# Selective scan: both channel halves in one two-bank PSUM tile, with softplus, delta times u and the turned copies as single operations

## The chip, the cores and the metric

The kernel runs on one core of a Trainium2 chip. The metric is device time in microseconds of one execution; three executions of the kernel before gave a median of 18506.04 us (18495.7 to 18506.94). The kernel has four layers in a row; the change lies in the scan of the last one.

## What is computed

The input is an image batch of 2 x 128 x 128 pixels with 128 channels. Layers 0 to 2 (window attention, a Fourier layer, a gated iteration) are not touched. Layer 3 is a selective scan in four directions over 256 channels. Cut to the part in question:

```
x_dbl = einsum('bkdl,kcd->bkcl', xs, x_proj_w)         # 4 directions k
dts, Bs, Cs = split(x_dbl, [8, 24], axis=2)
delta = softplus(einsum('bkrl,kdr->bkdl', dts, dt_proj_w) + dt_bias)
step:   h = exp(delta * A) * h + (delta * u) * B        # 16 states per channel
        y = sum over states of h * C
y = y + u * D;  the four directions are turned back and added
```

L is 16384 pixels, and each direction runs through them in its own order, two of them (k = 0, 1) forth and two (k = 2, 3) back.

## The kernel before, in words

`layer3_scan` (L1219) cuts each direction of each image into 32 parts of 512 pixels: 256 parts in all, in 8 blocks of 32, a block of "forth" parts (k below 2) and a block of "back" parts (k of 2 or 3) by turns. 256 channels times 16 states are 32 groups of 128 rows, so each part has 32 scans of 128 x 512. They are made in 8 slots of 4 (`tiles`, L1578): for each scan PE turns four 128 x 128 blocks of products `but` into a PSUM tile `ups` (L1591), and DVE scans it with the decay factors `da` into `hs` (L1599). `ups` has three buffers.

Around a scan slot g stands the rest of the recurrence, written out in the loop at L1623:

```
at(g, "head"); exponentials(g+1); kept(g-1); at(g, "mid")
products(g+2); weighted(g-1); tiles(g); sums(g-2); at(g, "end")
```

- `exponentials` (L1528): ACT makes `da`, four operations of 128 x 512.
- `kept` (L1605): ACT copies the last column of the four scans into `states`. It waits for the scans of slot g-1.
- `products` (L1540): `but` = delta times u, times B, 8 operations of 128 x 256, of which ACT does six or seven and POOL one or two.
- `weighted` (L1613): POOL multiplies `hs` by C in place, one operation of 128 x 2048.
- `sums` (L1563): PE sums over the states into two PSUM banks `yps`.

`in_order` (L114) ties every engine to the order in which this code issues, so nothing overtakes anything on its engine. Each part also has steps that run at fixed slots beside the scans of an earlier or later part. The list at L1508 gives (slot relative to the part's first, place in the slot, step); a place 0 to 3 is after that scan of the slot. By the slot of the eight in which they fall, with the engine that does the work:

| slot | steps |
|---|---|
| 6 | `project` (PE, `xdps`, places 1 and 2); `store` of a back part (ACT, head: two copies `yt<-ytps`, L1501) |
| 7 | `projected` (ACT, head: `xd`) |
| 0 | `turn_b` (PE, `btps`, 0), `ranks` 0 and 1 (PE, `dtps`, places 1 and 2) |
| 1 | `softplus_a` (ACT, head: two Abs out of `dtps`, L1366, and an Exp), `turned_b` (DVE, 0), `softplus_b` (DVE, 2), `skip` 0 (DVE, 3) |
| 2 | `softplus_c` (ACT, mid: Ln), `softplus_d` 0 and 1 (DVE, L1387, 0 and 1), `softplus_e` 0 and 1 (DVE, L1394, 2 and 3), `skip` 1 (DVE, 3) |
| 3 | `softplus_f` 0 and 1 (DVE, L1403, 0 and 1), `spread` (DMAs by SP, 2) |
| 4 | `turn` 0 and 1 (PE, `dltps`, L1430, 0 and 1) |
| 5 | `turned` 0 and 1 (DVE, `du` = `ut` times `dltps`, L1440, 0 and 1); `unturn` 0 and 1 of a back part (PE, `ytps`, L1491, places 2 and 3) |

PSUM has eight banks here: three `ups`, two `yps`, and three in `ps_m` (L1243). All small results (`xdps`, `btps`, the two `dtps`, the two `dltps`, the two `ytps`) are one-bank tiles of one tag in that pool, and take its three buffers by turns: a new tile waits until the last reader of the tile that had its buffer is done.

## Time and profile before

| | us |
|---|---|
| median of three executions | 18506.04 |
| the profiled execution | 18497.56 |
| its span, first to last instruction | 18495.8 |
| scan stage: first scan starts, last scan starts | 6302.4, 17972.4 |
| DVE, ACT, POOL busy between 8000 and 10000 (2000 us) | 1957.68, 1953.05, 1947.89 |
| PE busy in the same stretch | 1552.42 |

The profile page gives busy time by engine, by slices of the span and by group of instructions. The timeline lists instructions in order with their start, their length and, in brackets, the idle time of the engine before them and what ended it; a run of like instructions is one line. Lengths overlap: an instruction's tail lies under the next one's start, so what an instruction takes of its engine is the distance from its start to the next start, where the engine doesn't wait. In what follows that distance is called its step. The list of waits sums who waited for whom in a stretch.

### The profile page before, as it was taken

How to read it: one execution, taken by the hardware profiler on the slowest of the kernel's cores; microseconds unless marked ns; L12 is line 12 of the kernel's file. 1: busy time of each engine (PE TensorE's matmuls, PEld its weight loads, DVE VectorE, ACT ScalarE, POOL GpSimd, SP SyncE). 2: the span in 40 equal slices, each digit the busy share in tenths (PEclk: the TensorE clock that was granted, in tenths of full speed). 3: DMA queues.
4: the chain of work that ended last, by engine and by line, in shares of the span. 5: the costliest groups of instructions: out<-in, count | busy, mean ns of one | idle time of the engine just before them, and what ended most of it. 6: DMA issues, size and time to landing. Idle time of an engine off the chain costs nothing. (4 is left out here: it accounts for less than half of the span.)

```text
span 18495.8 us, 280256 instructions
## 1 busy us (share of the span) xinstructions
PE 14497.6 (78%) x98938; PEld 8455.1 (46%) x98938; DVE 15999.1 (87%) x20731; ACT 14932.9 (81%) x30141; POOL 11956.1 (65%) x6710
## 2 busy tenths in 40 slices
PE   7888888887567777777777777777777777777778
PEld 5665666674223344444444444444444444444445
DVE  6666666335888899999999999999999999999996
ACT  4665666333445799999999999999999999999984
POOL 0000000011000399999999999999999999999981
PEclk9999999889779899999999998999999989999999
DMA  2000000121114544444444454544444444455546
GB/s 49 23 23 22 16 16 16 55 72 55 49 48 147 174 119 119 118 126 126 127 114 119 120 128 126 126 118 116 120 126 127 126 122 115 116 122 128 132 129 191
DMA packets 1228553, 1861.32 MB, mean 101 GB/s; under 512 B 120781, under 2 KB 587469, under 8 KB 1224846
## 3 DMA queue, kind: packets, MB, share of 16 engines
q1 hardware_dynamic: 1157374, 1817.40, 37.2%
q10 hardware_dynamic: 69776, 26.00, 0.6%
q8 instruction: 785, 12.86, 0.3%
q14 instruction: 618, 5.06, 0.1%
HBM read 1398.48 MB, written 444.60 MB: 100 GB/s over the span
## 5 line engine op out<-in xcount | busy, mean ns | idle before, releaser
L1599 DVE TENSOR_TENSOR_SCAN hs<-da,states,ups 128x512 f32<-128x512 f32 x8192 | 9920.7, 1262 | 248.9 <-PE ups L1591 235.9
L1617 POOL TENSOR_TENSOR hs<-hs,cb 128x2048 f32<-128x2048 f32 x2048 | 9406.4, 4593 | 310.1 <-POOL but L1554 185.2
L1591 PE MATMUL ups<-ident,but 128*128 128x128 f32 x32768 | 5576.7, 301 | 2578.9 <-DVE hs L1599 1718.8
L1591 PEld LDWEIGHTS ups<-ident,but 128*128 128x128 f32 x32768 | 3873.7, 151 | 6179.9 <-DVE hs L1599 3526.1
L1559 ACT ACTIVATE but<-du,bt 128x256 f32<-128x256 f32 x12800 | 5328.7, 497 | 4.7 <-DVE du L1440 4.2
L1535 ACT ACTIVATE da<-db,na 128x512 f32<-128x512 f32 x8192 | 5224.1, 710 | 19.1 <-DMA db<-dd 17.8
L1573 PE MATMUL yps<-hs,sel 128*32 128x512 f32 x16384 | 2495.2, 685 | 60.7 <-POOL hs L1617 48.2
L1554 POOL TENSOR_TENSOR but<-du,bt 128x256 f32<-128x256 f32 x3584 | 2148.8, 620 | 15.2 <-DVE du L1440 15.2
L282 POOL TENSOR_TENSOR xres<-xres,rowb 128x256 f32<-128x256 f32 x128 | 93.2, 728 | 2641.3 <-DMA xres<-in_x 2512.5
L390 ACT COPY pT<-tps 128x512 f32<-128x512 f32 x1280 | 723.8, 586 | 1123.3 <-PE tps L385 1123.3
L385 PE MATMUL tps<-ident,s 128*128 128x128 f32 x8192 | 1180.8, 283 | 367.5 <-DVE pT L388 273.2
L358 DVE CUSTOM_DVE_ANT_0 s<-sps,relbias 128x512 f32<-128x512 f32 x2048 | 1321.6, 683 | 114.6 <-PE sps L342 109.2
L385 PEld LDWEIGHTS tps<-ident,s 128*128 128x128 f32 x8192 | 889.0, 142 | 898.8 <-issue 486.0
L370 ACT ACTIVATE s<-s,nm 128x1024 f32<-128x1024 f32 x1024 | 1163.5, 1137 | 85.3 <-DVE nm L368 82.1
L1130 POOL MEMSET xpad<- 128x34 f32 x8 | 1.3, 162 | 1242.5 <-PE xs L1021 1178.1
L1611 ACT COPY states<-hs 128x4 f32<-128x4 f32 x2048 | 380.9, 186 | 274.9 <-DVE hs L1599 274.7
L342 PE MATMUL sps<-kc,qT 32*128 32x512 f32 x4096 | 596.7, 650 | 0.8 <-DVE nm L358 0.8
L388 DVE COPY pT<-tps 128x512 f32<-128x512 f32 x768 | 526.6, 686 | 55.0 <-PE tps L385 54.5
L1573 PEld LDWEIGHTS yps<-hs,sel 128*32 128x32 f32 x16384 | 340.7, 114 | 486.0 <-issue 309.6
L1323 PE MATMUL xdps<-xc,xpw 128*40 128x512 f32 x1024 | 541.4, 611 | 12.3 <-POOL xd L1260 12.3
L1355 PE MATMUL dtps<-xd,dtw 65*128 65x512 f32 x1024 | 535.6, 605 | 0.0
L725 POOL TENSOR_TENSOR xr<-xr,row_ln_b 128x512 f32<-128x512 f32 x64 | 81.2, 1270 | 701.5 <-ACT acc L687 353.5
(286 smaller groups left out, 16784.7 us busy)
## 6 DMA issues: line engine op xcount, KB each, us to landing
db<-dd SPq DMA_DIRECT2D x1024, 512.0 KB
cb<-cd SPq DMA_DIRECT2D x1024, 256.0 KB
xc<-xs SPq DMA_DIRECT2D x256, 512.0 KB
dd<-dl SPq DMA_DIRECT2D x256, 512.0 KB
ut<-xst SPq DMA_DIRECT2D x128, 512.0 KB
yc<-ysb SPq DMA_DIRECT2D x128, 512.0 KB
yf<-yc SPq DMA_DIRECT2D x128, 512.0 KB
ys<-yt SPq DMA_DIRECT2D x128, 512.0 KB
```

The source lines that it names most:

```text
L342: nc.tensor.matmul(sps, v["qT"][hp, qt * P : (qt + 1) * P], kc[b, wh + g][hp, :, c0 : c0 + 32], start=True, stop=True,)
L358: nc.vector.tensor_tensor_reduce(v["s", qt][:, h, cols], v["sps", qt, g][h], bias[:, qt, h, cols], op0=ALU.add, op1=ALU.min, scale=-1.0, s ...
L370: nc.scalar.activation(s[:, h, :], s[:, h, :], AF.Exp, bias=nm[:, 2, h : h + 1], scale=-1.0, accum_out=v["sums"][:, qt, h : h + 1],)
L385: nc.tensor.transpose(tps[:, j, :], v["s", qt][:, h, k0 : k0 + P], cs.ident)
L390: nc.scalar.copy(dst, tps)
L1535: nc.scalar.activation(da[:, j, :], held[i]["db"][:, 4 * e + j, :], AF.Exp, scale=na[:, k, c : c + 1])
L1554: nc.gpsimd.tensor_tensor(but[:, j, :, n, :], du[:, tb], bt[:, tb, c : c + 1].unsqueeze(2).to_broadcast([P, 8, 32]), ALU.mult,)
L1559: nc.scalar.activation(but[:, j, :, n, :], du[:, tb], AF.Copy, scale=bt[:, tb, c : c + 1])
L1573: nc.tensor.matmul(v["yps"][e][32 * j : 32 * j + 32, :], sel, hs[:, j, :], start=(q == 0), stop=(q == 3),)
L1591: nc.tensor.transpose(ups[:, tb * P : (tb + 1) * P], v[("but", q, tb // 2)][:, tb % 2, 4 * e + j].rearrange("p n c -> p (n c)"), cs.ident,)
L1599: nc.vector.tensor_tensor_scan(o, a, u, state[:, c0 + j : c0 + j + 1], ALU.mult, ALU.add)
L1617: nc.gpsimd.tensor_tensor(hs, hs, v["cb"][:, s // 2, :].unsqueeze(1).to_broadcast([P, 4, T]), ALU.mult)
```

## The change

The pool `ps_m` gets one buffer for each tag instead of three. The tag "misc" keeps `xdps` and `btps`; a new tag "pair" holds one tile of two banks, shared by turns by `dtps`, `dltps` and `ytps`. The operations that ran once for each bank run once for both: `softplus_a`'s Abs, `softplus_d`, `_e`, `_f`, `turned` and `store`'s copy. Matmuls and transposes stay as they are, and write halves of the tile. Operations that came at places 0 and 1 (or 2 and 3) come at the first of them.

```diff
-        ps_m = pool("l3b_ps_m", 3, space=PSUM)
+        ps_m = pool("l3b_ps_m", 1, space=PSUM)
...
+        def two_banks(i, name):
+            return ps_m.tile([P, 2, T], F32, name=f"{name}_{tag_of(i)}", tag="pair")
...
         def ranks(e):
-                ps = ps_m.tile([P, T], F32, name=f"dtps_{tag_of(i)}_{e}", tag="misc")
+                if e == 0:
+                    v["dps"] = two_banks(i, "dtps")
                 nc.tensor.matmul(
-                    ps, dtw[:, k, e * P : (e + 1) * P], v["xd"], start=True, stop=True
-                )
-                v.setdefault("dps", []).append(ps)
+                    v["dps"][:, e], dtw[:, k, e * P : (e + 1) * P], v["xd"], start=True, stop=True
+                )
...
         def softplus_a(i):
-            for e in range(2):
-                nc.scalar.activation(ae[:, e, :], v["dps"][e], AF.Abs)
+            nc.scalar.activation(ae, v["dps"], AF.Abs)
             nc.scalar.activation(ae, ae, AF.Exp, scale=-1.0)
...
-                nc.vector.scalar_tensor_tensor(ps, ps, 0.0, v["ae"][:, e, :], ALU.max, ALU.add)
+            nc.vector.scalar_tensor_tensor(ps, ps, 0.0, v["ae"], ALU.max, ALU.add)
...
-                nc.vector.scalar_tensor_tensor(
-                    ps, v["up"][:, e, :], -1.0, ps, ALU.add, ALU.subtract
-                )
+            nc.vector.scalar_tensor_tensor(ps, v["up"], -1.0, ps, ALU.add, ALU.subtract)
...
-                nc.vector.tensor_tensor(dl, dl, v["dps"][e], ALU.subtract)
+            nc.vector.tensor_tensor(v["dl"], v["dl"], v["dps"], ALU.subtract)
...
         def turn(g):
-                tps = ps_m.tile([P, 2, 2, P], F32, name=f"dltps_{tag_of(i)}_{g}", tag="misc")
+                if g == 0:
+                    v["tps"] = two_banks(i, "dltps")
...
-        def turned(g):
-                nc.vector.tensor_tensor(
-                    v["du"][:, 2 * g : 2 * g + 2, :], v["ut"][:, 2 * g : 2 * g + 2, :],
-                    v["tps"][g].rearrange("p j e d -> p j (e d)"), ALU.mult,
-                )
+        def turned(i):
+            nc.vector.tensor_tensor(flat(v["du"]), flat(v["ut"]), flat(v["tps"]), ALU.mult)
...
         def unturn(g):
-                tps = ps_m.tile([P, 2, 2, P], F32, name=f"ytps_{tag_of(i)}_{g}", tag="misc")
+                if g == 0:
+                    v["ytps"] = two_banks(i, "ytps")
...
         def store(i):
-            for g in range(2):
-                nc.scalar.copy(
-                    yt[:, 2 * g : 2 * g + 2, :], v["ytps"][g].rearrange("p j e d -> p j (e d)")
-                )
+            nc.scalar.copy(flat(yt), flat(v["ytps"]))
             nc.sync.dma_start(pixels_of(i), yt)
...
-            (-6, "mid", softplus_c), (-6, 0, softplus_d(0)), (-6, 1, softplus_d(1)),
-            (-6, 2, softplus_e(0)), (-6, 3, softplus_e(1)),
-            (-5, 0, softplus_f(0)), (-5, 1, softplus_f(1)), (-5, 2, spread),
-            (-4, 0, turn(0)), (-4, 1, turn(1)), (-3, 0, turned(0)), (-3, 1, turned(1)),
+            (-6, "mid", softplus_c), (-6, 0, softplus_d), (-6, 2, softplus_e),
+            (-5, 0, softplus_f), (-5, 2, spread),
+            (-4, 0, turn(0)), (-4, 1, turn(1)), (-3, 0, turned),
```

In the order of issue this takes four DVE instructions out of every part (1024 in all) and 384 ACT instructions out of the scan (one Abs in each of 256 parts, one copy in each of 128 back parts). PE, POOL and SP keep their instructions and their order. Among the semaphore waits, the first transpose of `unturn(0)` gets a wait on DVE that it didn't have; before, `unturn(1)` had one.

More of the change, by code (lines that the diff above doesn't have):

```diff
@@ L1380, in softplus_c, with softplus_d, softplus_e, softplus_f @@
             v["dl"] = dl
-        def softplus_d(e):
-            def f(i):
-                v = held[i]
-                ps = v["dps"][e]
-                nc.vector.scalar_tensor_tensor(ps, ps, 0.0, v["ae"][:, e, :], ALU.max, ALU.add)
-            return f
-        def softplus_e(e):
-            def f(i):
-                v = held[i]
-                ps = v["dps"][e]
-                nc.vector.scalar_tensor_tensor(
-                    ps, v["up"][:, e, :], -1.0, ps, ALU.add, ALU.subtract
-                )
-            return f
-        def softplus_f(e):
-            def f(i):
-                v = held[i]
-                dl = v["dl"][:, e, :]
-                nc.vector.tensor_tensor(dl, dl, v["dps"][e], ALU.subtract)
-            return f
+        def softplus_d(i):
+            v = held[i]
+            ps = v["dps"]
+            nc.vector.scalar_tensor_tensor(ps, ps, 0.0, v["ae"], ALU.max, ALU.add)
+        def softplus_e(i):
+            v = held[i]
+            ps = v["dps"]
+            nc.vector.scalar_tensor_tensor(ps, v["up"], -1.0, ps, ALU.add, ALU.subtract)
+        def softplus_f(i):
+            v = held[i]
+            nc.vector.tensor_tensor(v["dl"], v["dl"], v["dps"], ALU.subtract)
         def spread(i):
@@ L1429, in f @@
                         p0 = (2 * g + j) * P
-                        nc.tensor.transpose(tps[:, j, e, :], v["dl"][:, e, p0 : p0 + P], cs.ident)
-                v.setdefault("tps", []).append(tps)
-            return f
-        def turned(g):
-            def f(i):
-                v = held[i]
-                if g == 0:
-                    v["du"] = two.tile([P, 4, 256], F32, name=f"du_{tag_of(i)}", tag="du")
-                nc.vector.tensor_tensor(
-                    v["du"][:, 2 * g : 2 * g + 2, :], v["ut"][:, 2 * g : 2 * g + 2, :],
-                    v["tps"][g].rearrange("p j e d -> p j (e d)"), ALU.mult,
-                )
-            return f
+                        nc.tensor.transpose(
+                            v["tps"][:, g, 256 * j + P * e : 256 * j + P * e + P],
+                            v["dl"][:, e, p0 : p0 + P], cs.ident,
+                        )
+            return f
+        def turned(i):
+            v = held[i]
+            v["du"] = two.tile([P, 4, 256], F32, name=f"du_{tag_of(i)}", tag="du")
+            flat = lambda a: a.rearrange("p t d -> p (t d)")
+            nc.vector.tensor_tensor(flat(v["du"]), flat(v["ut"]), flat(v["tps"]), ALU.mult)
         def load_forth(i):
@@ L1490, in f @@
                         p0 = (2 * g + j) * P
-                        nc.tensor.transpose(tps[:, j, e, :], v["ysb"][:, e, p0 : p0 + P], cs.ident)
-                v.setdefault("ytps", []).append(tps)
+                        nc.tensor.transpose(
+                            v["ytps"][:, g, 256 * j + P * e : 256 * j + P * e + P],
+                            v["ysb"][:, e, p0 : p0 + P], cs.ident,
+                        )
             return f
@@ L1499, in store @@
             yt = one.tile([P, 4, 256], F32, name=f"yt_{tag_of(i)}", tag="yt")
-            for g in range(2):
-                nc.scalar.copy(
-                    yt[:, 2 * g : 2 * g + 2, :], v["ytps"][g].rearrange("p j e d -> p j (e d)")
-                )
+            flat = lambda a: a.rearrange("p t d -> p (t d)")
+            nc.scalar.copy(flat(yt), flat(v["ytps"]))
             nc.sync.dma_start(pixels_of(i), yt)
```

## The prediction

> **What bounds the kernel now.** First the page: busy share by slices, and the costliest group.

> ```profile
> span 18495.8 us, 280256 instructions
> ...
> DVE  6666666335888899999999999999999999999996
> ACT  4665666333445799999999999999999999999984
> POOL 0000000011000399999999999999999999999981
> ...
> L1599 DVE TENSOR_TENSOR_SCAN hs<-da,states,ups 128x512 f32<-128x512 f32 x8192 | 9920.7, 1262 | 248.9 <-PE ups L1591 235.9
> ```

> From 6302 to 17972 us three engines are each over 90% busy: no single engine's sum sets the pace, their waits for each other do. So next the waits, ACT's in a stretch of back parts (7950 to 9300), then ACT's in a stretch of forth parts (9350 to 10700), then DVE's in the back parts. Columns: us in total, times, longest.

> ```profile
> ACT states L1611 <- DVE hs L1599: 23.0, 33, 1.6
> ```
> ```profile
> ACT states L1611 <- DVE hs L1599: 39.0, 61, 1.7
> ```
> ```profile
> DVE hs L1599 <- PE ups L1591: 34.7, 62, 1.7
> ```

> In the timeline of ACT the Ln of L1379 comes once a part; its starts are 45.4 to 45.6 us apart in back parts, 45.2 to 45.3 in forth parts (two or three parts of a block take 47.5). Back parts: ACT waits once a part, in `kept` of slot 3, and never elsewhere to speak of; DVE waits twice, before its first scans of slots 1 and 2. Now one back part's timeline, DVE, then ACT, then PE.

> ```profile
> 12013.59 0.30 DVE L1348 COPY bt<-btps 128x160 f32<-128x160 f32 x1
> 12013.81 2.44 DVE L1599 TENSOR_TENSOR_SCAN hs<-da,states,ups 128x512 f32<-128x512 f32 x2
> ...
> 12019.17 1.28 DVE L1599 TENSOR_TENSOR_SCAN hs<-da,states,ups 128x512 f32<-128x512 f32 x1 [0.56 <-PE ups L1591]
> ...
> 12022.13 0.67 DVE L1387 SCALAR_TENSOR_TENSOR dtps<-dtps,ae 128x512 f32<-128x512 f32 x1
> 12022.72 1.27 DVE L1599 TENSOR_TENSOR_SCAN hs<-da,states,ups 128x512 f32<-128x512 f32 x1
> ...
> 12038.73 0.66 DVE L1440 TENSOR_TENSOR du<-ut,dltps 128x512 f32<-128x512 f32 x1
> 12039.31 1.27 DVE L1599 TENSOR_TENSOR_SCAN hs<-da,states,ups 128x512 f32<-128x512 f32 x1
> ```
> ```profile
> 12032.87 0.20 ACT L1611 COPY states<-hs 128x4 f32<-128x4 f32 x1 [0.49 <-DVE hs L1599]
> ...
> 12037.83 0.18 ACT L1611 COPY states<-hs 128x4 f32<-128x4 f32 x1
> 12037.92 2.50 ACT L1559 ACTIVATE but<-du,bt 128x256 f32<-128x256 f32 x6
> 12040.33 1.04 ACT L1501 COPY yt<-ytps 128x512 f32<-128x512 f32 x2
> 12041.27 2.56 ACT L1535 ACTIVATE da<-db,na 128x512 f32<-128x512 f32 x4
> ```
> ```profile
> 12028.18 1.11 PE L1591 MATMUL ups<-ident,but 128*128 128x128 f32 x4 [1.71 <-DVE hs L1599]
> ...
> 12038.19 0.60 PE L1491 MATMUL ytps<-ident,ysb 128*128 128x128 f32 x4
> 12038.87 0.66 PE L1591 MATMUL ups<-ident,but 128*128 128x128 f32 x4
> 12039.44 0.66 PE L1491 MATMUL ytps<-ident,ysb 128*128 128x128 f32 x4
> ```

> The reader is to see **a ring**. DVE starts slot 2 at 12019.17, once PE has turned the products that ACT ended at 12018.69, and runs without a gap through slots 2 and 3, where most of its extra steps lie. ACT waits for the end of slot 3 (12032.87). From there ACT runs without a gap through slots 4 to 7, 0 and 1 (store, `xd`, Abs and Exp lie on that way) until it has made the next part's products for slot 2. So in a back part ACT's work from slot 4 to slot 1 and DVE's in slots 2 and 3 lie end to end. In forth parts, which have no store, ACT also waits in `kept` of slot 5, so the ring follows DVE through slots 2 to 5. POOL stands still about 1.1 us a part in both kinds, waiting for the others.

> [...] `bt`, 160 elements, has a step of 0.22 us (12013.59 to 12013.81), and a 512-element step is 0.59 us (12022.13 to 12022.72). That is 1.05 ns an element and 0.05 us fixed; I take 0.05[...]. [...] (12028.18: four transposes take 1.11 us after a pause, 0.60 to 0.66 otherwise).

> **The change part by part.** Slots are numbered 0 to 7, times are for one part.

> *d, e, f as single operations.* Three fixed shares of 0.05: 0.15 us off DVE in slots 2 and 3, on the ring in both kinds. [...] The merged d at place 0 and e at place 2 move one scan later by half a microsecond, but the ends of slots 2 and 3 come no later than now relative to ACT's `kept` (which starts 0.7 us or more after slot 2's end would be).

> *Abs as one.* 0.05 us off ACT at the head of slot 1, on the ring in both kinds. It waits for both `ranks`; the second ended at 12010.2, ACT came at 12011.58, so nothing is added. [...] bounds 0 and 0.1.

> *turned as one.* 0.05 us off DVE in slot 5: on the ring in forth parts. In back parts it enters below.

> *store's copy as one.* 0.05 us off ACT in slot 6, back parts, bounds 0 and 0.1.

> *"misc" with one buffer.* `xdps` (slot 6) is read in slot 7, `btps` (slot 0) in slot 1: never two alive, and each new one comes slots after the last reader. Nothing. The `xd` copy that hides it is a data dependence already.

> *"pair" with one tile.* `dtps` lives from slot 0 to `softplus_f` in slot 3; `dltps` from slot 4, which needs `softplus_f`'s data anyway, to `turned` in slot 5; `ytps` from `unturn` in slot 5 to the store at the head of 6; then slot 0 again. Only one meeting is tight: **`unturn(0)` must now wait for the whole of `turned`, in the same slot.** Before, the first `unturn` went to a free buffer at 12038.19, half a microsecond ahead of `turned`, and only the second had to follow `turned(0)`: it starts 0.05 us after that ends (12039.39, 12039.44). Behind the waiting transpose on PE's queue stand the transposes of scan 3 of slot 5, `unturn(1)`, slot 3's `sums` and slot 6's transposes; who waits for `unturn(1)` is ACT's store.

> The price, from the start of `turned`: its length is 0.66 + 0.54 (512 more elements at 1.05 ns) = 1.20; PE wakes after 0.05; three groups of four transposes follow, `unturn(0)`, `ups`, `unturn(1)`, at starts 0.57 apart (12038.87 to 12039.44) and 0.66 for the last: 1.80; ACT wakes after 0.05. In sum 3.10 us. Before, the store starts 1.71 us after `turned(0)` (the median of 105 back parts in the timeline, 1.59 to 1.97; 1.60 here). So ACT, which has no gap there now, stands still for about 3.10 - 1.71 = 1.39 us. DVE itself is not held up: it needs `ups` of scan 3 some 3.5 us after `turned` starts, and that is there after 2.5. ACT's delay is carried through slots 6, 7, 0 and 1 to the products for slot 2, with no gap in between to swallow it, and so into DVE's next slot 2. The 0.78 us that ACT waits now in slot 3 (23.0 us over the 29.7 parts of that stretch) doesn't swallow it either, for DVE's slots 2 and 3 begin later by the same amount. DVE's scans of slots 6 to 1 run up to 4 us ahead of ACT's `kept` (slot 0 ends at 12012.06, its `kept` comes at 12016.10), so what they lose is not on the ring.

> Sum for a back part: +1.39 - 0.15 (d, e, f) - 0.05 (Abs) - 0.05 (copy) = +1.14. For a forth part: -0.15 - 0.05 - 0.05 = -0.25. Times 128 each: +146 - 32 = **+114 us**. Against the profiled execution of 18497.56 (span 18495.8, 1.8 around it) that is 18612; the median shown is 8.5 higher, so 18620 on its scale.

> **The rivals.**
> - *Faster: the wait is covered.* Place: ACT at the head of slot 6. If the merged `turned` and PE's three groups end within 1.71 us of `turned`'s start instead of 3.10, or if ACT reaches the store as much later, nothing is added and all 256 parts save about 0.25 to 0.3: 18506 - 70 = 18436[...]. For it: DVE and ACT are both full, and 1024 and 384 instructions go. Against it: the order of PE's queue is fixed, and DVE's position in slot 5 is part of the same ring.
> - *No change: half of it is swallowed.* If ACT's 0.78 us of waiting in slot 3 does take up the delay, a back part gets 1.14 - 0.78 = 0.36 longer: +46 - 32 = +14, 18520. Against it: DVE waits for ACT's products at slot 2.
> - *Slower still: PE's clock.* PE would stand about 1.7 us before `unturn(0)`, as long as the pause at 12028.18, after which a group's step is 0.9 instead of 0.57. Three groups then cost 1.0 more: +128 us, 18748. For it: that very pause shows it; against it: after 1.11 us (12025.81) the group took 0.66, and PE is busier in slots 4 to 6 than in 2 and 3.

> **How the numbers follow.** The forecast is 18620, with a chance of 0.64; covered 0.08, half swallowed 0.08, slow PE 0.20. The range reaches from the half-swallowed case to the slow-PE case, 18520 to 18750. About 0.2% (37 us) is what a measurement here can tell from no change: faster 0.08, same 0.07, slower 0.85.

> **What would show it.** Right: ACT idle before L1495's copy by over 1 us, 128 times, released by PE `ytps`; PE idle before `ytps`, released by `du`; Ln starts 46.5 to 46.7 apart in back parts and about 45.0 in forth parts; steps of the merged operations near 1.13. Wrong: no idle time before that copy, or back parts no longer than 45.5 in spite of it; merged steps far from 1.13 would break the small terms. PE groups of 1.1 us in slot 5 would show the clock.

## The result, and the profile after

The changed kernel takes 18798.42 us (median; 18782.9 to 18802.81) against 18504.73 for the kernel before: ratio 1.016, 95% interval 1.0148 to 1.0173. The sign was forecast, the size was not: +294 us instead of +114, above the range.

The page of the changed kernel, with the granted PE clock:

```profile
span 18781.1 us, 278847 instructions
...
DVE  6666666336889899999999999999999999999986
ACT  4665666334446799999999999999999999999984
POOL 0000000011000599999999999999999999999981
PEclk9999999889779899888889988889988889888889
...
L1590 DVE TENSOR_TENSOR_SCAN hs<-da,states,ups 128x512 f32<-128x512 f32 x8192 | 9890.6, 1263 | 487.6 <-PE ups L1582 422.3
```

DVE's idle time before scans has doubled (248.9 to 487.6 us), and PE's clock row has more eights than before (mean granted clock of the span 0.894 against 0.919). ACT's waits, in the same two stretches as before: back parts (7950 to 9300), then forth parts (9350 to 10700), then DVE's in the back parts.

```profile
ACT states L1602 <- DVE hs L1590: 52.7, 51, 1.6
ACT yt L1495 <- PE ytps L1483: 40.6, 28, 2.6
```
```profile
ACT states L1602 <- DVE hs L1590: 28.6, 60, 0.7
```
```profile
DVE hs L1590 <- PE ups L1582: 75.1, 116, 1.6
```

Forth parts have less waiting than before (39.0 to 28.6). In back parts there is the wait that was forecast, 28 times, 1.45 us on average, in front of the store's copy. But ACT's wait for DVE has also doubled (23.0 to 52.7), and so has DVE's for PE (34.7 to 75.1); neither was forecast. One back part, the forecast wait first: DVE, PE, ACT.

```profile
12121.44 1.19 DVE L1435 TENSOR_TENSOR du<-ut,dltps 128x1024 f32<-128x1024 f32 x1
12122.56 4.79 DVE L1590 TENSOR_TENSOR_SCAN hs<-da,states,ups 128x512 f32<-128x512 f32 x4
```
```profile
12122.69 0.66 PE L1483 MATMUL ytps<-ident,ysb 128*128 128x128 f32 x4 [1.63 <-DVE du L1435]
```
```profile
12124.26 1.01 ACT L1495 COPY yt<-ytps 128x1024 f32<-128x1024 f32 x1 [1.19 <-PE ytps L1483]
```

`turned` has a step of 1.12 us; PE stands 1.63 us until it ends; the copy comes 2.82 us after `turned` starts, where it came 1.71 us after (the median) before. Then what was not forecast, in the slots just ahead of it and behind the store of the part before: PE from the end of slot 7 into slot 0, DVE in slots 0 and 1, POOL in slot 1, and ACT in `kept` of slots 1, 2 and 3.

```profile
12085.04 0.33 PE L1582 MATMUL ups<-ident,but 128*128 128x128 f32 x1 [1.20 <-ACT but L1550]
...
12086.16 1.68 PE L1359 MATMUL dtps<-xd,dtw 65*128 65x512 f32 x2
...
12088.49 1.92 PE L1359 MATMUL dtps<-xd,dtw 65*128 65x512 f32 x2
```
```profile
12088.81 1.28 DVE L1590 TENSOR_TENSOR_SCAN hs<-da,states,ups 128x512 f32<-128x512 f32 x1 [0.87 <-ACT but L1550]
12091.37 1.28 DVE L1590 TENSOR_TENSOR_SCAN hs<-da,states,ups 128x512 f32<-128x512 f32 x1 [1.28 <-PE ups L1582]
12093.91 1.28 DVE L1590 TENSOR_TENSOR_SCAN hs<-da,states,ups 128x512 f32<-128x512 f32 x1 [1.26 <-ACT da L1526]
...
12097.68 2.65 DVE L1375 TENSOR_SCALAR up<-ae 128x1024 f32<-128x1024 f32 x1
```
```profile
12095.22 4.55 POOL L1608 TENSOR_TENSOR hs<-hs,cb 128x2048 f32<-128x2048 f32 x1 [1.58 <-issue]
```
```profile
12101.55 0.20 ACT L1602 COPY states<-hs 128x4 f32<-128x4 f32 x1 [1.59 <-DVE hs L1590]
...
12109.10 0.20 ACT L1602 COPY states<-hs 128x4 f32<-128x4 f32 x1 [1.54 <-DVE hs L1590]
...
12115.51 0.20 ACT L1602 COPY states<-hs 128x4 f32<-128x4 f32 x1 [0.96 <-DVE hs L1590]
```

ACT is late, so PE waits 1.20 us for the products of slot 0, and then its matmuls take 1.68 and 1.92 us where a pair takes 1.02 at full clock. Slot 0, with `btps`, two `dtps` and `sums`, leaves PE no room (in the kernel before, PE was busy for all of the 5.16 us from the first scan of slot 0 to that of slot 1, in the mean of inner back parts), and DVE waits for it, 1.28 us. So DVE comes to `softplus_b` (`up`) after POOL has begun `weighted`, and `up` lasts 2.65 us instead of 0.67: until 12100.33, which is 0.56 us after POOL's operation ended at 12099.77. POOL's next operations then last 1.63 us instead of 1.18. I call these two things together, PE's slow matmuls in slot 0 and the long `up`, **the cascade**.

### The profile page after: what moved, and what is told of

It reads as the page before. It is cut to its first block, busy times and chain, and to the rows that moved or that the text cites. A ratio compares the mean times of both kernels' runs of the same rounds, so it can differ in the third digit from the quotient of the medians.

```text
span 18781.1 us, 278847 instructions
## 1 busy us (share of the span) xinstructions
PE 14794.4 (79%) x98938; PEld 8651.5 (46%) x98938; DVE 16049.5 (85%) x19707; ACT 14937.1 (80%) x29757; POOL 11979.8 (64%) x6710
## 3 DMA queue, kind: packets, MB, share of 16 engines
q14 instruction: 607, 4.97, 0.1%
## 5 line engine op out<-in xcount | busy, mean ns | idle before, releaser
L1590 DVE TENSOR_TENSOR_SCAN hs<-da,states,ups 128x512 f32<-128x512 f32 x8192 | 9890.6, 1263 | 487.6 <-PE ups L1582 422.3
L1582 PE MATMUL ups<-ident,but 128*128 128x128 f32 x32768 | 5658.7, 306 | 2353.7 <-DVE hs L1590 1551.8
L1582 PEld LDWEIGHTS ups<-ident,but 128*128 128x128 f32 x32768 | 4007.1, 154 | 6027.0 <-DVE hs L1590 3513.7
L1564 PE MATMUL yps<-hs,sel 128*32 128x512 f32 x16384 | 2648.5, 724 | 64.4 <-POOL hs L1608 64.4
L1359 PE MATMUL dtps<-xd,dtw 65*128 65x512 f32 x1024 | 596.4, 667 | 0.0
```

The lines of the kernel that those rows point to most:

```text
L1564: nc.tensor.matmul(v["yps"][e][32 * j : 32 * j + 32, :], sel, hs[:, j, :], start=(q == 0), stop=(q == 3),)
L1582: nc.tensor.transpose(ups[:, tb * P : (tb + 1) * P], v[("but", q, tb // 2)][:, tb % 2, 4 * e + j].rearrange("p n c -> p (n c)"), cs.ident,)
L1590: nc.vector.tensor_tensor_scan(o, a, u, state[:, c0 + j : c0 + j + 1], ALU.mult, ALU.add)
```

## The experiments

All numbers by part come from the trace of each run: the distance of ACT's successive Ln starts, for 116 inner parts of each kind (29 of each block of 32; the first three are left out). "Long `up`" counts inner back parts with `softplus_b` over 1 us, "slow PE" those with a matmul of `dtps` over 0.6 us. "PE pause" is a mean over inner back parts: PE's waits, of 0.15 us or more, before its instructions that start in the last 4 us up to `btps` of slot 0.

| kernel | forth us | back us | long `up` | slow PE | PE pause us | median us |
|---|---|---|---|---|---|---|
| before | 45.51 | 45.64 | 4 | 2 | 1.28 | 18504.73 |
| changed | 44.99 | 48.53 | 53 | 53 | 1.65 | 18798.42 |
| e1 unturn a slot later | 45.00 | 47.96 | 54 | 54 | 1.80 | 18720.82 |
| e2 turned earlier | 45.59 | 47.39 | 41 | 41 | 1.61 | 18724.23 |
| e3 shared, not merged | 45.42 | 47.54 | 27 | 25 | 1.56 | 18720.71 |
| e4 fill before unturn | 45.03 | 50.43 | 101 | 101 | 1.80 | 19015.02 |
| e5 unturn(0) in its own bank | 44.97 | 45.23 | 0 | 0 | 1.32 | 18383.04 |
| e6 fill in slot 7 | 44.97 | 46.94 | 3 | 0 | 0.95 | 18586.1 |
| e7 ACT delayed in before | 45.60 | 50.21 | 88 | 88 | 1.78 | 19083.7 |
| e8 another form of `up` | 45.35 | 48.49 | all over 1 | 45 | 1.57 | 18872.18 |
| e9 `up` later, on e5 | 47.78 | 48.00 | all, 4.1 us | 0 | 1.31 | 19085.78 |

The kernel before, run beside them, had medians of 18492.37 (e1 to e4), 18523.12 (e5 to e8) and 18529.72 (e9). The first theory was that the new wait is all; the rival, that the merged operations do it.

**e1**, the unturn and store moved away from `turned`:

```diff
-            (13, 2, unturn(0)), (13, 3, unturn(1)),
-            (14, "head", store),
+            (14, 0, unturn(0)), (14, 3, unturn(1)),
+            (15, "head", store),
...
-            for g in range(-15, slots + 7):
+            for g in range(-15, slots + 8):
```

> The changed kernel with all its merged operations, but unturn at places 0 and 3 of slot 6 and store at the head of slot 7, one slot later, where turned has long ended. Theory (the wait of unturn(0) for turned on the shared tile is the whole cause): no ACT idle before the yt copy, back parts about 45.3 us, forth parts 45.0, time about 18440 (18506 - 256 x 0.27), faster than before. Rival (the two-bank operations, or the longer pauses that they give PE, are the cause): back parts stay above 47, time 18700 to 18800.

Ratio 1.0121 (1.0104 to 1.0138). The wait before the copy is gone, the time is not: a failure for the theory as expected, and within the rival's range. The trace shows why it isn't a clean removal. The 32 undisturbed back parts take 45.86 to 46.02 us: ACT now waits 0.5 us for DVE at the end of slot 5, as in forth parts, and makes the copy (0.9 us) after that instead of inside that slack: 45.0 + 0.9. ACT is late in slot 7 again, by another way, PE's pause is 1.80 us, and the cascade is there in 54 parts.

**e2**, `turned` moved instead:

```diff
-            (-4, 0, turn(0)), (-4, 1, turn(1)), (-3, 0, turned),
+            (-4, 0, turn(0)), (-4, 1, turn(1)), (-4, 3, turned),
```

> The changed kernel with turned at place 3 of slot 4 instead of place 0 of slot 5; unturn and store stay. Theory: unturn(0) comes two scans after turned, no wait is left, time about 18440 as with unturn moved. Rival (merged operations are the cause): 18700 to 18800. A third outcome, between 18440 and 18520, would say that turned in slot 4 delays the end of that slot for ACT.

Ratio 1.0124 (1.0108 to 1.0139). It didn't remove what it should: PE runs three `ups` buffers ahead of DVE, so it comes to `unturn(0)` just when `turned` runs, and still waits 0.46 us for it; and scan 0 of slot 5, now behind `turned`, frees the buffer for scan 3's transposes 1.1 us later, which `unturn(1)` stands behind. The store still waited 0.73 us a part. Undecided.

**e3**, the kernel before with the change's buffers alone:

```diff
-        ps_m = pool("l3b_ps_m", 3, space=PSUM)
+        ps_m = pool("l3b_ps_m", 1, space=PSUM)
...
-                ps = ps_m.tile([P, T], F32, name=f"dtps_{tag_of(i)}_{e}", tag="misc")
+                ps = ps_m.tile([P, T], F32, name=f"dtps_{tag_of(i)}_{e}", tag=f"pair{e}")
...
```

(`dltps` and `ytps` likewise with `pair{g}`.)

> The kernel before with its single-bank operations at their old places, and only the buffers of the change: one for xdps and btps, one for each half of dtps, dltps and ytps. Nothing is merged. Theory (the shared buffer is the cause): unturn(0) waits for turned(0) and unturn(1) for turned(1), the store comes 3.1 us after turned(0) starts instead of 1.7, back parts 47 to 51 as in the changed kernel, forth parts 45.3 as before; time about 18830. Rival (merged operations are the cause): 18506, no change.

Ratio 1.0123 (1.0108 to 1.0138): +228 us with nothing merged. The rival's "no change" is out; sharing is enough for most of the loss. ACT's waits in the stretch 7950 to 9300 have

```profile
ACT yt L1501 <- PE ytps L1491: 26.4, 28, 1.4
```

but not where I expected it: the first of the two copies comes 1.71 us after `turned(0)` starts, as before, and the wait stands before the second, 0.96 us in the mean of 126 parts where the changed kernel has 1.38. So ACT is delayed less, and the cascade comes in 27 parts instead of 53; the time is 110 us below what I expected.

**e4**, work for PE in the pause before `unturn(0)`:

```diff
+            t = ps_m.tile([P, 4, P], F32, name=f"fill_{tag_of(i)}", tag="misc")
+            for j in range(9):
+                nc.tensor.transpose(t[:, j % 4, :], cs.group, cs.ident)
...
-            (13, 2, unturn(0)), (13, 3, unturn(1)),
+            (13, 2, fill), (13, 2, unturn(0)), (13, 3, unturn(1)),
```

> The changed kernel plus nine transposes of a constant into an unused PSUM tile just before unturn(0) of back parts, where PE stands for 1.6 us; they add nothing to what is computed. Theory with PE's clock as the amplifier of that pause: the store still waits about 1.2 us, but PE keeps its clock in slots 5 to 0, softplus_b no longer collides with POOL, back parts are 46.6 to 46.9 throughout, time about 18620. Rival (the clock has other pauses as its cause, or the collision follows from ACT's delay alone): back parts stay at 48 to 49, time 18770 to 18820.

Ratio 1.0276 (1.0255 to 1.0296), the worst yet. The fill does what it is for at its own place: the store comes 2.80 to 2.82 us after `turned` starts in 126 parts, and waits 1.11 us. But that pause is not the one that lowers the clock of slot 0: the cascade now strikes in 101 of 116 parts. PE's pause before slot 0 is 1.80 us here. Why it is longer than in the changed kernel, though the store waits less, stays open. That the cascade strikes nearly everywhere fits its length: of the 85 struck parts that follow a struck one, 75 take 50.9 to 51.5 us, fifteen times the 3.413 us of the grid on which the changed kernel's clock records lie (51.2; see the last section), so the next part would meet that grid at nearly the same point.

The theory needed a second part: ACT's delay, by whatever cause, lengthens PE's pause at the end of slot 7, and that pause sets off the cascade. The next four runs test it.

**e5**, the shared buffer avoided, all else in place. `misc` is idle from slot 1 to slot 6, so `unturn(0)` can have it:

```diff
-                if g == 0:
-                    v["ytps"] = two_banks(i, "ytps")
+                if g == 0:
+                    tps = ps_m.tile([P, T], F32, name=f"ytps_{tag_of(i)}", tag="misc")
+                else:
+                    tps = two_banks(i, "ytps")[:, 0]
...
-            nc.scalar.copy(flat(yt), flat(v["ytps"]))
+            for g in range(2):
+                nc.scalar.copy(
+                    yt[:, 2 * g : 2 * g + 2, :].rearrange("p t d -> p (t d)"), v["ytps"][g]
+                )
```

> The changed kernel, but unturn(0) goes to the idle one-bank tag misc and only unturn(1) to a bank of the shared pair, at the old places; store copies the two banks one by one, right behind each other. Nothing else moves. Theory (ACT's delay at the store, from the shared buffer, starts the loss): the wait before the store shrinks from 1.4 us to 0.3 or less, the parts in which softplus_b takes over 1 us nearly vanish, back parts about 45.5, time about 18470. Rival (the merged DVE operations start it, through longer pauses of PE): back parts stay at 47.5 to 48.5, time 18700 to 18800.

Ratio 0.9922 (0.9906 to 0.9939): faster than both kernels. ACT's only wait in the stretch 7950 to 9300 is

```profile
ACT states L1607 <- DVE hs L1595: 11.6, 31, 0.5
```

so nothing is left before the copies, no part has a long `up`, and back parts take 45.23. `unturn(1)` still waits 0.46 us for `turned`, but ACT makes the first copy meanwhile. All merged DVE operations and their places are as in the changed kernel: the rival that blames them is out. The store's copy is split again here; e3, with a split copy and the shared buffer, still has the wait, so the split alone doesn't do it. Whether the bank alone would, no run shows.

**e6**, work for PE in the other pause:

```diff
-            (14, "head", store),
+            (14, "head", store), (15, "end", fill),
```

(`fill` as in e4, with eight transposes.)

> The changed kernel plus eight transposes of a constant at the end of slot 7 after back parts, where PE stands about 1.2 us until ACT's products come; they add nothing to what is computed. Theory (that pause lowers PE's clock for slot 0): dtps at full clock in nearly all parts, softplus_b over 1 us in under 10 of 116 back parts, back parts 46.7 to 47.6, time about 18640. Rival (the clock of slot 0 is set by earlier pauses, or PE is too full there already): count and time stay, 18750 to 18900.

Ratio 1.0033 (1.002 to 1.0046). The store's wait is still there (1.58 us), but after the fill PE's last wait is short and `dtps` is at full clock in every inner part:

```profile
12290.74 0.33 PE L1589 MATMUL ups<-ident,but 128*128 128x128 f32 x1 [0.48 <-ACT but L1557]
...
12291.86 1.02 PE L1359 MATMUL dtps<-xd,dtw 65*128 65x512 f32 x2
```

Three parts have a long `up`, and back parts take 46.94. This run is the change without the cascade: 212 us of the changed kernel's time go (18798 to 18586), and 63 us above the kernel before beside it are left.

**e7**, the kernel before with ACT delayed by two more copies (a step of 2.18 us for the four, 0.94 for the two):

```diff
-            for g in range(2):
+            for g in (0, 1, 1, 1):
```

> The kernel before with its three-buffer PSUM pool and unmerged operations; only the second copy of store is made three times, which puts about 1.15 us more on ACT in slot 6 of back parts and holds up nothing else. Theory (any delay of ACT there lengthens the ring by its own size and, past about 1 us, lowers PE's clock and makes softplus_b meet POOL): back parts 47.0 to 48.5 with softplus_b over 1 us in a quarter or more of them, forth parts 45.3, time 18700 to 18850. Rival (only the ring, no cascade): back parts 46.7, time 18506 + 128 x 1.15 = 18653. Rival (ACT has slack there): 18506 to 18560.

Ratio 1.0301 (1.0285 to 1.0316). No buffer is shared and nothing is merged, and the cascade comes in 88 of 116 parts; the shortest back part is 46.79, 1.2 us more than usual. The cascade needs only ACT's delay. It cost more than I expected: 4.6 us a part.

**e8**, `softplus_b` as a plain addition of two tensors:

```diff
-            nc.vector.tensor_scalar(up, v["ae"], 1.0, None, ALU.add)
+            nc.vector.tensor_tensor(
+                up, v["ae"], cs.ones[:, 0:1].unsqueeze(2).to_broadcast([P, 2, T]), ALU.add
+            )
```

> The changed kernel with softplus_b as an addition of a broadcast tile of ones, 1024 elements at the rate of the other two-input DVE operations (about 1.2 us) instead of 0.67. Theory (softplus_b's 2.5 us in half of the back parts is a meeting with POOL's weighted, and only its fast form has it): its length is 1.2 us in every part, forth parts 45.5, back parts 47.5 to 48.0 instead of 48.5, time 18770 to 18830. Rival (it is long for another reason): some still take 2.5 us or more, back parts above 49, time above 18900.

Ratio 1.0186 (1.0171 to 1.0201). Missed: the operation takes 1.20 us in the 71 back parts with PE at full clock, but 1.63 in the mean of forth parts and 3.06 in the 45 back parts with slow PE. This form is held up beside POOL too: all 141 instances over 1.3 us end 1.08 us after the end of an operation of POOL (91 times `but`, 50 times `weighted`), about its own length. It doesn't tell what the first form's length comes from.

**e9** does, on e5, where nothing is late:

```diff
-            (-7, "head", softplus_a), (-7, 0, turned_b), (-7, 2, softplus_b),
+            (-7, "head", softplus_a), (-7, 0, turned_b), (-7, 3, softplus_b),
```

> The version with unturn(0) in the one-bank tag (18383 us, back parts 45.2, forth parts 45.0, no part with softplus_b over 1 us), but softplus_b at place 3 of slot 1 instead of place 2, so one scan later, when POOL is in its 4.6 us weighted of slot 0. It prices the meeting of softplus_b and POOL by itself. Theory (softplus_b waits until POOL's operation ends, on the ring): softplus_b 2 to 3.5 us long in nearly every part of both kinds, every part longer by 1 to 2.5 us, time 18640 to 19000, with dtps at full clock. Rival (softplus_b is long only where PE's slow clock has upset the part): it stays at 0.67, time within 50 us of 18383.

Ratio 1.0297 (1.0279 to 1.0314), 703 us slower than e5. Instances of `up` (lengths least, median, most), then one with POOL's operation:

```profile
L1375 DVE TENSOR_SCALAR up<-ae x256: 693/4098/4115, 6291.7 to 18491.5; 128x1024 f32<-128x1024 f32 x128
```
```profile
13030.91 4.10 DVE L1375 TENSOR_SCALAR up<-ae 128x1024 f32<-128x1024 f32 x1
```
```profile
13029.93 4.52 POOL L1613 TENSOR_TENSOR hs<-hs,cb 128x2048 f32<-128x2048 f32 x1 [0.50 <-POOL but L1550]
```

POOL's operation ends at 13034.45, `up` at 13035.01, 0.56 later, about its own length, as if it did its work only after POOL was through. The same holds in every run but e8: all 677 instances of this form over 1 us end 0.55 to 0.56 us after the end of a `weighted`. `dtps` is at full clock in every inner part, and both kinds lengthen by 2.8 us. The meeting costs by itself, without any slow PE. Why POOL's instruction holds DVE up, no run shows. `up` has one input in SBUF and a step of 0.58 us for its 1024 elements, e8's form has two and takes 1.20 us, and both were held up. The merged d, e and f, with one input in PSUM, stayed at 1.18 to 1.23 us in all 256 parts.

## Why the prediction was wrong

- *d, e, f, Abs and `turned` as single operations: right.* A forth part shows them alone: the median went from 45.32 to 45.02, -0.30 against -0.25 forecast; the merged step is 1.12 (forecast 1.13). For ACT 0.05 us an operation was my estimate: from the first Abs to the Exp it is 1.04 us where it was 1.09, 0.05 saved, and the store's one copy has a step of 0.91 where the two took 0.94, 0.03 saved. The mean went down by 0.52: before, a few disturbed parts and those that follow them lift it to 45.51; after, there are none.
- *"misc" with one buffer, nothing: right*; no wait on it shows.
- *The wait of `unturn(0)`: right in place; the size came out right by luck.* Forecast 1.39 us of ACT idle time; measured 1.38, the mean of 126 waits (173.4 us; the stage's last one, of 11.0, is left out). Two errors cancel in it. The two starts behind a wait, taken as 0.05 us each, are not among them: PE began 0.055 us after `turned` ended, ACT 0.037 us after `unturn(1)` ended (medians of 127). In 81 parts PE's granted clock is full from the end of `turned` to the store: the store comes 2.82 us after `turned` starts, not 3.10, and ACT waits 1.06. I had taken 0.57 us for a group's step, from 12038.87 to 12039.44, but that second group had waited for `turned(0)`; the steps are 0.50 and 0.43, and 0.60 for the last. In the other 45 parts the clock is at half for some of that time: the store comes 3.26 to 4.11 us after, and ACT waits 1.94. The sum for a back part was +1.14; e6, which has this wait (1.58) without the cascade, has 46.94 - 45.64 = 1.30. Over 128 parts of each kind e6's profile is 18595.1 - 18495.8 = 99 us longer, forecast 114.
- *What failed* is the sentence that DVE's scans of slots 6 to 1 run up to 4 us ahead of ACT, "so what they lose is not on the ring". They lose more than the slack: in the part shown, DVE waits 0.87, 1.28 and 1.26 us in slots 0 and 1, for PE or for ACT, and `up` takes 2.0 us more than 0.67: 5.4 us in all. ACT then waits for DVE in `kept` of slots 1, 2 and 3, where before it waited in slot 3 alone. Changed minus e6 in back parts: 48.53 - 46.94 = 1.59 us; times 128 = 204 us, about the gap between the two runs (212) and that between the measured loss and the forecast (294 - 114 = 180).
- *The rival of PE's slow clock had the right agent, but not the place where it costs most.* I priced it at the pause before `unturn(0)` in slot 5, with 1.0 us for three groups. It did come there, in 45 of 126 parts, with 0.44 to 1.29 us. But e4, which takes it away there, made things worse; e6, which fills the pause in slot 7, removed the large loss. I had not asked what ACT's own delay does to PE at its next wait for ACT.
- *The second half of the cascade stood in the profile of before.* `softplus_b` was already long in some parts:

```profile
L1373 DVE TENSOR_SCALAR up<-ae x256: 662/669/4969, 6277.4 to 17895.6; 128x1024 f32<-128x1024 f32 x128
```

Its median is 0.67 us and its longest 4.97. The two or three parts of about 47.5 us in a block, which I noted and passed over, are these and the ones behind them: 20 parts take over 46.5 us, ten with a long `up` and the ten that follow. In e9, where `up` comes one scan later in every part, 255 of its 256 instances meet POOL's operation; I had taken lateness there as free.
- *The rivals that forecast no loss:* the wait was neither covered nor half swallowed.

What stays open: how much of the 1.59 us is PE and how much is `up`. They come together in all 53 parts, and no run has the slow PE without long `up`. The other way about, e9 has a long `up` alone, 4.1 us in every inner part, and pays 2.8 us a part for it.

## What to carry to other kernels

Merging operations over banks costs buffers, and a buffer shared by two tiles puts one tile's reader in front of the other's writer (here PE stood 1.63 us for it): look where the two live in the same slot, and give the one that is written there a bank that is idle just then (e5, with the store's copy split again: -0.78%, where the merges with the shared tile cost +1.6%). Slack isn't free when it is used up (e7: 1.24 us more of ACT's work cost 4.6 us a part): before calling an engine's delay harmless, ask what its next customers do while they wait, and what they then run into. The longest instance of an operation, beside its median (here 4.97 us and 0.67), can show a meeting of two engines that a mean hides.
